# Two transformer layers in one kernel: the order of the last norms, the slot scores and three output operations

## The chip, the cores and the metric

One core of a Trainium2 chip. The time is device microseconds of one launch; the kernel before took 2937.34 us (median of three runs, 2937.07 to 2941.98). One more execution was taken with a profile, and all instruction times below are from it.

## What is computed

Two layers on x (32 sequences of 64 tokens, width 512). Each layer adds a cross attention to a context (32 query heads, 8 key/value heads of 128) and a feed-forward part. The change lies in the second layer's feed-forward part, a small memory with 128 slots:

```python
query = h @ Wq.T                                   # h = layernorm'ed x, width 512 -> 64
router_scores = (query @ Wr.T) @ (aux_keys @ Wr.T).T / sqrt(48) + log_rel
top 8 of 128 slots by router_scores
w = softmax over those 8 of (query @ aux_keys.T / 8 + log_rel)
aux_out = (w @ aux_values) @ Wvd.T @ Wvu.T
norm_var = log1p(var(h)) / (mean over all tokens of log1p(var(h)) + 1e-6)
learned = gelu(h @ Wu1.T + bu1) @ Wu2.T + bu2
u = clip(norm_var * 0.5 + sigmoid(learned) * 2.5, 0, 5)
gate = sigmoid(gate_w1 * clip((u - 0.5) / 1.5, 0, 1) + gate_bias), 0 where below 0.05
out = x + h + gate * aux_out                       # x before the norm, from the residual
```

The mean of the log variances goes over all tokens, so no gate can be finished before the last norm has its variances.

## The kernel before

The 2048 tokens lie in four chunks (c = 0 to 3) of 512 tokens, each four tiles of 128 tokens. x stays in SBUF as `x_sb[c]`. An attention runs over 32 steps (g, c): eight key/value heads g, and in each the four chunks. A step projects keys, values and queries of the next step, forms the scores S, the softmax, the values po and the output products O. Large products are done by a seven-product scheme on quarter blocks (line 186 for all of them): `product` issues eight matmuls (two for each 128x256 piece at 32-bit data), and `left_sums` and `right_sums` form the extra blocks on GpSimd (lines 166 to 177).

A tile scheduler orders the instructions of each engine from priorities and dependencies; each engine then runs its own list strictly in order, and semaphores tie the lists together. Buffers come from pools: `mm_tile` has six PSUM banks, `st_tile` one double bank, used by the attention scores S and also by the slot scores pr; `m2_tile` has four SBUF buffers.

In the output products, `output_first` forms product 1 into a bank x and product 2 into another, and adds each to the residual on VectorE (`out_add`, line 592). `output_rest` forms product 4, then product 6 on top of bank x, then 5 and 3, then product 7 on top of bank x again, each followed by its add. So product 6 can only be written when the first add has read bank x. Between these adds the softmax of the next step is worked off: S scaled (L504, VectorE), mask added (L514, GpSimd), maximum over keys r2x (L525), m1x, its spread mb (L278), subtraction (L538), exponential (L540, ScalarE), sums r2s, and the multiplication on GpSimd (L546). The scaling needs qr, a power of 128x20 values on GpSimd (L229), from sums pm that TensorE folds. GpSimd's list in such a step is qr, four left sums of oT, two mask adds.

In the last three steps of the second attention (7, 1) to (7, 3), chunk c - 1 of the residual is complete (`joined`, `norm_stats`), and behind the query projection come `norm_apply(c, "d", mem_each)` and `mem_weights(c)`; the fourth chunk follows behind the last step. `norm_apply` goes over four tiles: xnd by a tensor_scalar on VectorE (L251), four transposes xtd on TensorE (L256), a copy to xnT on ScalarE (L260). With `each`, `mem_each` then takes that tile's variance (bn_stats L1002, bn_aggr L1003) on VectorE and adds xnd into x_sb on GpSimd (L1004).

`mem_weights` projects xnT to pqy (`project`, L1014), copies it to qy, projects xnT to pu (the gate's hidden layer, two halves of 256 tokens), and then does the slot scores pr (L1031) by four matmuls. The gelu gT (L1035) reads pu, pl (L1038) is its product with Wu2, lrn (L1041) the copy of that. On VectorE the two slot-score operations L1046 and L1049 read pr; max and match_replace (L1054, L1055), left (L1057) and copy_predicated (L1058) keep the eight best. `mem_softmax` takes their maximum mmx (L1069, L1070) and the exponentials (L1072, ScalarE). `mem_values` transposes them (pwt) and multiplies with the folded values (paux). In the last chunk `behind` is `mem_mean`: the log variances (L1101), their sum over all tokens by a product with ones (plv, L1103), and its reciprocal (L1104 to L1106).

`mem_gate` forms the gates, "a" for chunks 0 to 2 and "b" for chunk 3. `mem_out` divides by the softmax sums and issues for each tile one scalar_tensor_tensor, o = aux * gate + x (L1148), and its transfer out (L1151) on SP's queue. Chunks 0 to 2 keep aux in SBUF, chunk 3 in PSUM.

Of the kernel before, what the change touches and what calls it, by code (L numbers as in the profile page):

```python
# [15 lines left out]
ALU = mybir.AluOpType  # L16
AX = mybir.AxisListType

P = 128
# [11 lines left out]
TT = CH // P  # L31
# [5 lines left out]
BOT = 64  # L37
# [7 lines left out]
def tile_xattn_ffn_2_layers(ctx: ExitStack, tc: tile.TileContext, a: dict, out: bass.AP):  # L45
    nc = tc.nc
# [12 lines left out]
    def mm_tile(name):  # L59
        return psp.tile([P, CH], F32, tag="mm", name=name)  # L60

    def st_tile(name):
        return psp.tile([P, 2, CH], F32, tag="st", name=name, bufs=1)

    def m2_tile(name):
        return ap_.tile([P, CH], F32, tag="m2", name=name, bufs=4)
# [4 lines left out]
    def q_tile(name):  # L71
        return ap_.tile([P, 4, CH], F32, tag="q", name=name, bufs=1)
# [20 lines left out]
    x_sb, xnT = [], []  # L93
# [77 lines left out]
    def right_sums(t):  # L171
        b = [t[:, k] for k in range(NBLK)]
        tt = nc.gpsimd.tensor_tensor
        tt(b[4], b[1], b[0], ALU.subtract)
        tt(b[5], b[3], b[4], ALU.subtract)
        tt(b[1], b[3], b[1], ALU.subtract)
        tt(b[6], b[2], b[5], ALU.subtract)
# [68 lines left out]
    def norm_apply(c, name, each=None):  # L246

        mv, rs = norms[c]
        for t in range(TT):
            xn = m2_tile(f"xn{name}{c}_{t}")  # L250
            ins = nc.vector.tensor_scalar(  # L251
                xn, x_sb[c][:, t, :], mv[:, t, 0:1], rs[:, t : t + 1], ALU.subtract, ALU.mult
            )
            pt = mm_tile(f"xt{name}{c}_{t}")
            for k in range(KT):
                nc.tensor.transpose(  # L256
                    pt[:, k * P : (k + 1) * P], xn[:, k * P : (k + 1) * P], ident
                )
            at = (t % 2) * P
            nc.scalar.copy(  # L260
                xnT[c][:, t // 2 : 4 : 2, :, at : at + P],
                pt.rearrange("p (j k t) -> p j k t", j=2, k=2),
            )
            if each is not None:
                each(c, t, xn)
        if each is None:
            right_sums(xnT[c])
        return ins.ins

# [13 lines left out]
    def key_blocks(kT):  # L283

        return kT.rearrange("p (f e j k) -> p f e j k", f=NH, j=4, e=KH)

    class Attention:
# [174 lines left out]
        def scores(self, g, c, kT, qT):  # L462
            n = f"{self.L}_{g}_{c}"
            kT = key_blocks(kT)
            st = st_tile(f"S{n}")
            s5 = st.rearrange("p f (e w) -> p f e w", e=KH)
            for f in range(NH):
                for e in range(KH):
                    for j in range(4):
                        nc.tensor.matmul(  # L470
                            s5[j * KB : (j + 1) * KB, f, e],
                            kT[:, f, e, j],
                            qT[:, f * 4 + j].rearrange("p h q -> p (h q)"),
                            start=True,
                            stop=True,
                        )
            return st
# [454 lines left out]
    mem = {}  # L932
# [73 lines left out]
    def blocks(c, k):  # L1006
        return xnT[c][:, k].rearrange("p h w -> p (h w)")

    def mem_weights(c, behind=lambda: None):

        def project(ps, w):
            for half in range(2):
                for k in range(KT):
                    nc.tensor.matmul(  # L1014
                        ps[:, half * HC : (half + 1) * HC],
                        w[:, k, :],
                        xnT[c][:, 2 * (k // 2) + half, k % 2, :],
                        start=(k == 0),
                        stop=(k == KT - 1),
                    )  # L1020

        py = mm_tile(f"pqy_{c}")
        project(py[0:BOT], mem["wq"])
        qy = m2_tile(f"qy{c}")
        nc.vector.tensor_copy(qy[0:BOT, :], py[0:BOT, :])
        p = mm_tile(f"pu1_{c}")
        project(p, mem["wu1"])
        behind()
        pr = st_tile(f"pr{c}").rearrange("p j (t n) -> p (j t) n", t=2)
        for t in range(TT):  # L1030
            nc.tensor.matmul(  # L1031
                pr[:, t, :], qy[0:BOT, t * P : (t + 1) * P], mem["m2"], start=True, stop=True
            )
        gT = m2_tile(f"gT{c}")
        nc.scalar.activation(gT, p, AF.Gelu_apprx_tanh, bias=mem["bu1"])  # L1035
        pl = mm_tile(f"pl{c}")
        for t in range(TT):
            nc.tensor.matmul(  # L1038
                pl[:, t : t + 1], gT[:, t * P : (t + 1) * P], mem["wu2"], start=True, stop=True
            )  # L1040
        nc.vector.tensor_copy(mem["lrn"][:, c * TT : (c + 1) * TT], pl[:, 0:TT])  # L1041
        bc = [P, TT, NSLOT]
        lr = mem["lr"].unsqueeze(1).to_broadcast(bc)

        r, rr, att = (blocks(c, k).rearrange("p (t n) -> p t n", t=TT) for k in (4, 5, 6))
        nc.vector.scalar_tensor_tensor(  # L1046
            r, pr[:, :, 0:NSLOT], 1.0 / math.sqrt(RDIM), lr, ALU.mult, ALU.add
        )
        nc.vector.scalar_tensor_tensor(  # L1049
            att, pr[:, :, NSLOT : 2 * NSLOT], 1.0 / math.sqrt(BOT), lr, ALU.mult, ALU.add  # L1050
        )
        top = sm.tile([P, TT, 8], F32, tag="top", name=f"top{c}")
        for t in range(TT):
            nc.vector.max(top[:, t, :], r[:, t, :])  # L1054
            nc.vector.match_replace(rr[:, t, :], top[:, t, :], r[:, t, :], -BIG)  # L1055
        left = sm.tile([P, TT, NSLOT], U8, tag="left", name=f"left{c}", bufs=1)
        nc.vector.tensor_tensor(left, rr, r, ALU.is_equal)  # L1057
        nc.vector.copy_predicated(  # L1058
            att, left, neg[:, 1:2].unsqueeze(2).to_broadcast(bc)
        )  # L1060
        mem["att", c] = att
# [71 lines left out]
    def mem_out(name, c0, c1):  # L1133
        gate = mem["gate", name]
        sums = mem["sums"][:, c0 * TT : c1 * TT]
        nc.vector.reciprocal(sums, sums)
        nc.vector.tensor_tensor(gate, gate, sums, ALU.mult)
        for c in range(c0, c1):
            o4 = (
                q_tile(f"o{c}")  # L1140
                if c == 0
                else (o_tile if c == 1 else w_tile)(f"o{c}")[:, 0:4].rearrange("p b h w -> p b (h w)")
            )
            for t in range(TT):
                g = c * TT + t
                col = g - c0 * TT
                o = o4[:, t, :]
                nc.vector.scalar_tensor_tensor(  # L1148
                    o, mem["aux", c, t], gate[:, col : col + 1], x_sb[c][:, t, :], ALU.mult, ALU.add
                )  # L1150
                nc.sync.dma_start(out[g * P : (g + 1) * P, :], o)  # L1151


# [16 lines left out]

    norm_stats(0, "a")
    first = norm_apply(0, "a")
    att0.start()

    def behind_first(c):
        with tc.issue_after(first):
            mask_flags(c)
            if c == 0:
                key_weight()
            if c < last:  # L1180
                load_mask(c + 1)
                norm_stats(c + 1, "a")
                norm_apply(c + 1, "a")
# [6 lines left out]
        },  # L1190
        lambda c: norm_stats(c, "b"),
        lambda c: norm_apply(c, "b"),
        tail=lambda: (ffn_load_down(0), ffn_dequant(0)),
        late={(g, c): [lambda: next(pieces, None)] for g in range(1, NKV - 1) for c in range(NCH)},
    )

    def load_second():
# [14 lines left out]
        {(0, 1): [lambda: norm_apply(last, "c")], (1, 0): [lambda: mem_constants(att1.loaded)]},  # L1212
        lambda c: (mem_values(c - 1) if c > 0 else None, norm_stats(c, "d")),
        lambda c: (norm_apply(c, "d", mem_each), mem_weights(c)),
        lambda c: mem_softmax(c, att1.copied),
    )
    norm_apply(last, "d", mem_each)
    mem_weights(last, mem_mean)
    mem_gate("a", 0, last)
    mem_softmax(last)  # L1220
    mem_values(last)
    mem_gate("b", last, NCH)
    mem_out("a", 0, last)
    mem_out("b", last, NCH)


# [77 lines left out]
```

## Time and profile before

| | |
|---|---|
| Median of three runs | 2937.34 us |
| Profiled execution, its own time | 2943.32 us |
| Its span, first to last instruction | 2941.5 us |
| Mean granted TensorE clock | 0.987 |
| TensorE busy | 2838.8 us, 97% |
| VectorE busy | 1812.1 us, 62% |
| GpSimd busy | 1283.9 us, 44% |
| ScalarE busy | 820.2 us, 28% |
| First xnd of chunks 0, 1, 2, 3 | 2755.94, 2816.95, 2864.97, 2905.33 us |
| First and last L1148 start | 2926.42 us; the last ends at 2938.32 us |

Read it as one execution: starts count from the first instruction. PE is TensorE's matmuls, PEld its weight loads, DVE VectorE, ACT ScalarE, POOL GpSimd, SPq the queue that issues transfers. In a timeline a row gives the start, the length, the instruction (output <- inputs, partitions x elements) and how many of them; in brackets the idle time before it and what ended that. Line numbers are those of the kernel before.

### The profile page before, as it was taken

The page shows a single profiled execution, that of the slowest core. Times are in us where ns is not written, and L with a number is a line of the kernel's source. Part 1 is how long each engine was busy: PE and PEld are TensorE (multiplying, and loading weights), DVE is VectorE, ACT ScalarE, POOL GpSimd, SP SyncE. Part 2 cuts the span into 40 slices and gives each one's busy share as a digit, 9 for nine tenths or more (in the row PEclk, how much of TensorE's full clock was granted, in tenths as well). Part 3 has the DMA queues.
Part 4 walks back from the last instruction along what each step waited for, and adds up shares of the span by engine and source line. Part 5 has one row for each costly group of instructions (what it writes and reads, how often), then busy time and mean ns, then how long its engine had stood idle before and what let it go on. Part 6 is the DMA issues. An engine that isn't in the chain of part 4 may idle for free.

```text
span 2941.5 us, 40415 instructions
## 1 busy us (share of the span) xinstructions
PE 2838.8 (97%) x16502; PEld 2217.1 (75%) x16502; DVE 1812.1 (62%) x2752; ACT 820.2 (28%) x1397; POOL 1283.9 (44%) x932
## 2 busy tenths in 40 slices
PE   7999999999999999899999999999999999999987
PEld 5878787778887787676666677777777777787765
DVE  7667777777777766544433665555555555555565
ACT  3323333333333333211111222222222222222232
POOL 5544545454545455411222444444445353535432
PEclk9999999999999999899999999999999999999998
DMA  4111111111111111000000102120202020201001
GB/s 159 40 44 44 52 45 51 49 60 51 45 52 44 51 44 58 23 22 22 20 8 17 36 29 67 34 65 30 65 29 65 30 65 29 65 31 64 15 1 58
DMA packets 103807, 130.71 MB, mean 44 GB/s; under 512 B 8725, under 2 KB 65165, under 8 KB 103623
## 3 DMA queue, kind: packets, MB, share of 16 engines
q1 hardware_dynamic: 103047, 127.09, 13.3%
q8 instruction: 130, 2.13, 0.3%
q10 hardware_dynamic: 576, 1.05, 0.1%
q14 instruction: 54, 0.44, 0.1%
HBM read 123.92 MB, written 4.19 MB: 44 GB/s over the span
## 4 chain that ended last, share of the span: by engine, by line
PE 80%; DVE 12%; ACT 3%; issue 2%; POOL 2%; DMA 0%; DVEq 0%; ACTq 0%; POOLq 0%
PE P L186 30%; PE O L186 22%; PE pv L369 8%; PE pk L339 6%; PE pd L896 5%; PE S L470 4%; DVE part L425 2%; PE po L566 2%; DVE x L592 2%; DVE qT L419 1%; ACT q L421 1%; ACT rq L384 1%; DVE S L493 1%; PE pqy L1014 1%; DVE r2x L525 1%
## 5 line engine op out<-in xcount | busy, mean ns | idle before, releaser
L186 PE MATMUL P<-xnT,wq 128*128 128x256 f32 x3584 | 799.2, 382 | 23.4 <-ACT h L209 21.9
L186 PE MATMUL O<-wo,oT 128*128 128x256 f32 x3584 | 803.8, 382 | 4.2 <-ACT oT L574 3.3
L186 PEld LDWEIGHTS P<-xnT,wq 128*128 128x128 f32 x3584 | 678.8, 191 | 159.2 <-issue 39.2
L186 PEld LDWEIGHTS O<-wo,oT 128*128 128x128 f32 x3584 | 671.4, 190 | 118.0 <-issue 22.1
L592 DVE TENSOR_TENSOR x<-x,O 128x512 f32<-128x512 f32 (+1 forms) x448 | 368.5, 823 | 145.6 <-PE O L186 145.1
L546 POOL TENSOR_TENSOR s<-s,ib 128x512 f32<-128x512 f32 x128 | 169.6, 1347 | 489.0 <-DVE ib L278 480.5
L209 ACT COPY h<-P 128x512 f32<-128x512 f32 (+1 forms) x352 | 200.1, 573 | 365.4 <-PE P L186 354.5
L388 POOL TENSOR_TENSOR qT<-h,rq 128x512 f32<-128x512 f32 x128 | 175.4, 1370 | 277.1 <-DVE rq L387 267.2
L186 PE MATMUL P<-xnT,wgu 128*128 128x256 f32 (+1 forms) x1232 | 273.8, 382 | 0.0
L540 ACT ACTIVATE s<-s 128x1024 f32<-128x1024 f32 x64 | 67.7, 1057 | 708.1 <-DVE s L538 708.1
L186 PEld LDWEIGHTS P<-xnT,wgu 128*128 128x128 f32 (+1 forms) x1232 | 228.0, 187 | 47.1 <-issue 7.4
L229 POOL TENSOR_TENSOR qr<-qs,nhalf 128x20 f32<-128x20 f32 x32 | 113.4, 3543 | 335.0 <-DVE qs L458 335.0
L369 PE MATMUL pv<-wkv,ctxT 128*128 128x128 f32 x1984 | 238.0, 278 | 3.0 <-DVE h L401 1.7
L369 PEld LDWEIGHTS pv<-wkv,ctxT 128*128 128x128 f32 x1984 | 226.2, 192 | 14.0 <-issue 8.6
L384 ACT COPY rq<-h 64x512 f32<-64x512 f32 x256 | 157.9, 617 | 245.3 <-DVE h L401 242.9
L339 PE MATMUL pk<-ctxT,wkv 128*128 128x512 f32 x496 | 223.1, 592 | 0.0
L419 DVE TENSOR_TENSOR qT<-h,P 128x512 f32<-128x512 f32 x128 | 83.9, 674 | 170.4 <-PE P L186 170.4
L885 POOL TENSOR_TENSOR hT<-h,h 128x512 f32<-128x512 f32 (+1 forms) x48 | 55.6, 1179 | 283.4 <-DVE h L878 263.7
L339 PEld LDWEIGHTS pk<-ctxT,wkv 128*128 128x128 f32 x496 | 94.1, 190 | 92.9 <-issue 89.9
L896 PE MATMUL pd<-wd,hT 128*128 128x512 f32 (+1 forms) x352 | 155.0, 592 | 0.0
L386 DVE TENSOR_TENSOR h<-h,cosT 128x512 f32<-128x512 f32 x128 | 90.0, 703 | 105.0 <-ACT rq L384 105.0
L878 DVE TENSOR_TENSOR h<-h,P 128x512 f32<-128x512 f32 (+1 forms) x96 | 59.6, 640 | 151.9 <-PE P L186 103.7
(235 smaller groups left out, 3234.4 us busy)
## 6 DMA issues: line engine op xcount, KB each, us to landing
ctxT<-in_ctxT SPq DMA_DIRECT2D x62, 1024.0 KB
wq<-in_L_wq SPq DMA_DIRECT2D x32, 256.0 KB
wo<-in_L_wo SPq DMA_DIRECT2D x32, 256.0 KB
wq<-in_L_wqT SPq DMA_DIRECT2D x32, 256.0 KB
wo<-in_L_woT SPq DMA_DIRECT2D x32, 256.0 KB
wgu<-in_qweight_gu SPq DMA_DIRECT2D x40, 128.0 KB
out<-o SPq DMA_DIRECT2D x16, 256.0 KB
x<-in_x SPq DMA_DIRECT2D x12, 256.0 KB
```

The lines of the kernel that those rows point to most:

```text
L186: nc.tensor.matmul(pv[0:w, m, :], left[:, l, k, m * P : m * P + w], right[:, r, k, :], start=(first and m == 0 and k == 0), stop=(k == 1), ...
L209: nc.scalar.copy(t[size], ps[size])
L229: nc.gpsimd.tensor_tensor(dst, src, nhalf[:, : src.shape[-1]], ALU.pow)
L339: nc.tensor.matmul(ps, wkv[:, k, 0, :], ctxT[:, k, :], start=(k == 0), stop=(k == KT - 1))
L369: nc.tensor.matmul(ps[:, t * HD : (t + 1) * HD], ctxT[:, k, t * P : (t + 1) * P], wkv[:, k, 1, :], start=(k == 0), stop=(k == KT - 1),)
L384: nc.scalar.copy(t[lo:hi, 1], src[HD - hi : HD - lo])
L388: nc.gpsimd.tensor_tensor(dst(None), dst(x), dst(t[:, 1]), ALU.add)
L419: nc.vector.tensor_tensor(q, xv, yv, ALU.add)
L470: nc.tensor.matmul(s5[j * KB : (j + 1) * KB, f, e], kT[:, f, e, j], qT[:, f * 4 + j].rearrange("p h q -> p (h q)"), start=True, stop=True,)
L546: nc.gpsimd.tensor_tensor(sv[:, f], sv[:, f], ib[:, f * W : (f + 1) * W].unsqueeze(1).to_broadcast([P, KH, W]), ALU.mult,)
L592: self.added = nc.vector.tensor_tensor(dst, dst, src, ALU.add).ins
L896: nc.tensor.matmul(p, hT[0:w_, t, tk * P : (tk + 1) * P], wd[i][0:w_, t, :], start=(t == 0), stop=(t == len(tiles) - 1),)
```

## The change

Three edits. In `norm_apply` with `each`, all four tiles are scaled, transposed and copied first, and `each` is called for the four tiles behind that loop. In `mem_weights`, `behind()` and the four matmuls of the slot scores pr are issued between the two halves of pu. In `mem_out`, tile 0 of chunks 0, 1 and 2 is formed on GpSimd by two operations, aux * gate in place and then the addition of x, in place of one operation on VectorE.

```diff
     def norm_apply(c, name, each=None):
 
         mv, rs = norms[c]
+        tiles = []
         for t in range(TT):
             xn = m2_tile(f"xn{name}{c}_{t}")
...
-            if each is not None:
+            tiles.append(xn)
+        if each is not None:
+            for t, xn in enumerate(tiles):
                 each(c, t, xn)
-        if each is None:
+        else:
             right_sums(xnT[c])
         return ins.ins
...
-        def project(ps, w):
+        def project(ps, w, between=None):
             for half in range(2):
+                if half == 1 and between is not None:
+                    between()
                 for k in range(KT):
...
         p = mm_tile(f"pu1_{c}")
-        project(p, mem["wu1"])
-        behind()
         pr = st_tile(f"pr{c}").rearrange("p j (t n) -> p (j t) n", t=2)
-        for t in range(TT):
-            nc.tensor.matmul(
-                pr[:, t, :], qy[0:BOT, t * P : (t + 1) * P], mem["m2"], start=True, stop=True
-            )
+
+        def scores():
+            behind()
+            for t in range(TT):
+                nc.tensor.matmul(
+                    pr[:, t, :], qy[0:BOT, t * P : (t + 1) * P], mem["m2"], start=True, stop=True
+                )
+
+        project(p, mem["wu1"], scores)
...
-                nc.vector.scalar_tensor_tensor(
-                    o, mem["aux", c, t], gate[:, col : col + 1], x_sb[c][:, t, :], ALU.mult, ALU.add
-                )
+                if name == "a" and t == 0:
+
+                    aux = mem["aux", c, t]
+                    nc.gpsimd.tensor_scalar(aux, aux, gate[:, col : col + 1], None, ALU.mult)
+                    nc.gpsimd.tensor_tensor(o, aux, x_sb[c][:, t, :], ALU.add)
+                else:
+                    nc.vector.scalar_tensor_tensor(
+                        o, mem["aux", c, t], gate[:, col : col + 1], x_sb[c][:, t, :],
+                        ALU.mult, ALU.add,
+                    )
                 nc.sync.dma_start(out[g * P : (g + 1) * P, :], o)
```

## The prediction

> **What bounds the kernel.** First the page: the totals say that TensorE works nearly all the time.
>
> ```profile
> span 2941.5 us, 40415 instructions
> PE 2838.8 (97%) x16502; PEld 2217.1 (75%) x16502; DVE 1812.1 (62%) x2752; ACT 820.2 (28%) x1397; POOL 1283.9 (44%) x932
> ```
>
> The change touches only the last 186 us (2755.9 to 2941.5), so I read that stretch by the chain of waits and by the timeline of each engine. First, the stage behind chunk 0's last norm (TensorE, VectorE, GpSimd; columns: start, length, instruction, then idle before it):
>
> ```profile
> 2774.14 2.01 PE L566 MATMUL po<-s,v 32*128 32x256 f32 x32
> 2780.02 3.62 PE L186 MATMUL O<-wo,oT 128*128 128x256 f32 x16
> 2783.57 1.93 PE L470 MATMUL S<-qT,kT 128*32 128x256 f32 x32
> 2785.43 8.93 PE L186 MATMUL O<-wo,oT 128*128 128x256 f32 x40
> ...
> 2783.62 1.44 DVE L592 TENSOR_TENSOR x<-x,O 128x512 f32<-128x512 f32 x2
> 2790.49 1.25 DVE L525 TRANSPOSE_TENSOR_REDUCE r2x<-s 128x32 f32<-128x1024 f32 x1 [2.34 <-POOL s L514]
> ...
> 2779.41 3.54 POOL L229 TENSOR_TENSOR qr<-qs,nhalf 128x20 f32<-128x20 f32 x1 [16.82 <-DVE qs L458]
> 2787.96 2.49 POOL L514 TENSOR_TENSOR s<-s,mask 128x512 f32<-128x512 f32 x2
> ```
>
> TensorE has no gap in the 40 matmuls of products 4, 6, 5, 3, 7. VectorE adds products 1 and 2 at 2783.62, long before r2x, which waits for GpSimd's chain: qr, four left sums of oT (1.27 each), two mask adds. Chunk 0's stage is TensorE's; in chunk 1, 61.2 us later, the chain of waits runs through this GpSimd chain and VectorE's list behind r2x, and TensorE idles 4.64 us before the next transposes.
>
> Next, the timelines of VectorE and GpSimd where they collide:
>
> ```profile
> 421.35 0.74 DVE L745 SCALAR_TENSOR_TENSOR scales_down<-scales_down,pidx 30x512 f32<-30x512 bf16 x1
> 422.13 1.38 DVE L744 CAST scales_down<-scales_down 30x512 bf16<-30x512 f32 x1
> 423.54 1.64 DVE L745 SCALAR_TENSOR_TENSOR scales_down<-scales_down,pidx 30x512 f32<-30x512 bf16 x1
> ...
> 421.49 3.15 POOL L546 TENSOR_TENSOR s<-s,ib 128x512 f32<-128x512 f32 x2 [8.95 <-DVE ib L278]
> ```
>
> The same scalar_tensor_tensor takes 0.74 or, issued under a GpSimd operation, 1.64, ending 0.54 after it; the cast is held likewise (0.42 alone at 420.16). GpSimd's pair takes 3.15 instead of 2.5. They take turns, one operation each.
>
> Last, TensorE's clock and the end, by windows (length, PE, PEld, DVE, ACT, POOL busy, PEclk, DMA share, GB/s):
>
> ```profile
> 2886.00:2887.00 1.00, 0.14 (x1) 0.14 (x2) 0.93 (x3) 1.00 (x3) 0.00 (x0) 1.00 0.00 0
> 2888.00:2889.00 1.00, 1.00 (x3) 0.82 (x4) 0.02 (x1) 1.00 (x5) 1.00 (x1) 0.50 0.00 0
> 2934.00:2935.00 1.00, 0.18 (x1) 0.00 (x0) 1.00 (x3) 0.00 (x0) 0.00 (x0) 1.00 0.98 375
> ```
>
> After an idle 2.07 us (2884.8 to 2886.9) the granted clock falls to 0.50 for 3.4 us (2887.9 to 2891.3). In the tail the output transfers already fill 16 engines at 375 GB/s.
>
> **The change, part by part.** The order of the built instructions (no times) decides more than the diff: the scheduler moves three further things. (a) S of the next step (16 matmuls) goes from behind products 1 and 2 to right behind the gate's projection pu. (b) On VectorE, behind the S scaling (L504), come r2x, m1x and mb, and only then the add of product 1; before, the adds of 1, 2 and 4 preceded r2x. (c) The copy lrn, which waits for pl, moves from before the second slot-score operation (L1049) to behind the top-k list. ScalarE's order is unchanged.
>
> *Chunk 0: +6.2.* The norm first: tile 1's scaling now waits for GpSimd's x add of tile 0, tile 3's for that of tile 1; the last scaling ends about 2760.2 instead of 2761.24. Half clock until 2765 makes that 1.0 worth 0.5 in pqy's end (4.93 there, 3.67 in chunk 3 at full clock). From pqy's end at 2766.75: first half of pu, pr, second half (3.66 + 1.94), S 1.86 (covers the gelu's 2.1 of table load and activation but 0.2), pl 1.0, po 1.95, pm 0.25: qs at 2777.75. The top-k list, ready for lrn at 2775.2, is ahead of pl's end. So qr starts 1.4 earlier (2778.0) and r2x with it, at 2789.05. TensorE: pv 3.7, products 1 and 2 3.6, product 4 1.8: done at 2786.7. Product 6 writes product 1's bank and must wait for its add: r2x 1.2, m1x 0.1, mb 0.75, add 0.6, so 2791.7. New stall: 5.0, with pwt, paux and the next pk queued behind it on TensorE. Less 0.5 and less the 0.27 idle before pl that S now covers (I take 0 to 0.3): 4.5 net. The clock will fall in a 5 us gap, as it did after 2.07; running on at half speed for 1.7 to 5.1 us costs 0.85 to 2.55; I take 1.7. Nothing later absorbs it: pk, P and the quarter adds of step (7,3) follow TensorE up to xnd.
>
> *Chunk 1: +1.0.* Same stall, but here VectorE's list sets the end. r2x 1.4 earlier; behind it stand adds 1, 2 and 4 too (3 x 0.6), and the exp's wait (1.2) covers one 0.6 add instead of a 1.2 one: 2.4 longer. Bounds 0 to 2.
>
> *Chunk 2: -0.2.* Xnds 0 to 2 and one statistic come first; but GpSimd's add waits when xnd 1 ends, so by the turns above xnd 2 and xnd 3 are held one add each and the last ends as before: 0 (if VectorE keeps its place, -1.1). With the stall gone before it, TensorE idles about 1 us instead of 4.64 and should be warm: pqy 3.67 for 5.42, -1.8. Against that, nothing stands between pu and pl but the gelu now: pl, po, the oT copies on ScalarE and product 1 come 1.1 later. The new 2.15 gap could also pull the clock down under po, by the rows above: 0 to 1.5, I take 0.5.
>
> Here a rule can be weighed. The row says that 2.07 us idle cost the clock. The Trainium skill (TensorE: Matmul & The Clock Gate, Part 1) says that only gaps of over some 3.4 us do; that disagrees with the row. By the rule the 0.5 is 0 and the sum 0.5 lower; I keep the row.
>
> *Chunk 3: -1.5.* The norm 0 as in chunk 2. The slot scores start 1.75 earlier (pr behind pu's first half and plv), but pl ends at 2922.85 instead of 2920.71 and lrn now stands before the maximum: mmx starts at 2923.0 instead of 2924.92. The b gate's offset and its exp now lie behind mmx (0.3). The a gates are ready 1.5 earlier.
>
> *Outputs: +2.2.* VectorE loses three of twelve L1148 (3 x 0.66), GpSimd gains three scalings and three adds. An add is 1.27 (all 128x512 rows). A one-input scaling is in no row: below, 0.66 (identity's affine select, 0.30 for 128 elements, against 0.59 for a 192-element add, scaled by length); above, the add's 1.27. I take 0.66, the row with one input. Each L1148 reads two SBUF tensors, as L745 does, so they take turns: L1148 0.65, then six turns of (GpSimd 0.66 or 1.2, L1148 0.54), two more L1148, 0.5 for the b gate, four of 0.68: the last ends 14.1 behind the gate; before it was 11.9 (2926.4 to 2938.3). So +2.2, +4.0 by the upper price. SP's queue gives the same: its second transfer now waits for GpSimd's third operation (4.3 behind the gate), and the other 13 or 14 stand behind that; 15 transfers at 0.7 from 5.2, and the 1.5 from last byte to end, give 17.2 against 15.1. Without turns, and with the cheap scaling, it would be +0.4.
>
> The Trainium skill (GPSIMD Engine Reference, 3.1) gives 769 ns for a one-input loop over 512 elements. By it the tail would be +2.5.
>
> **Sum:** 6.2 + 1.0 - 0.2 - 1.5 + 2.2 = +7.7. On the profiled execution's 2943.32 (1.8 beyond its span) that is 2951.0. That execution lies 6.0 above the median of the runs shown, 2937.34, whose spread is 2937.07 to 2941.98; so I put the same difference on the median: 2945.0.
>
> **Rivals.**
> *Not slower: product 6 isn't held.* Place: its wait on the add. It decides if r2x can come 5.0 us sooner against TensorE. For it: the gate's path is shorter. Against: qr 3.54, four sums and two mask adds are fixed rows between qs and r2x, and VectorE's listed order puts the add behind. Price: chunk 0 becomes -0.4, chunk 1 -1.4; the idle before chunk 2 and its half clock come back (+1.8): sum +0.5, 2937.8.
> *Turns go VectorE's way.* If xnds run on while GpSimd waits, each norm gains 1.1 (0.5 in chunk 0): sum about +4.5, 2941.8. For: xnd 2 at 2758.09 went ahead of an add issued 0.07 later. Against: L387 at 439.65, right behind L386, was held 1.1.
> *All dear.* Scaling at 1.27 (+1.8), no warm clock in chunk 2 (+1.8): +11.3, and slow products in chunk 1 0.8 more: 2949.4.
>
> **How the numbers follow.** Forecast 0.62 (own range +4.5 to +11), not held 0.10, VectorE's turns 0.18, all dear 0.10. Of the forecast 0.5, all of the dear case and a third of the VectorE case lie beyond 5.9 us, 0.2%, about what a measurement of this kernel tells from no change: slower 0.67, same 0.29, faster 0.04. The range leaves out most of "not held" and the far end of the dear: 2938.8 to 2950.5.
>
> **What would show it.** Right: an idle of about 5 us before the second of the O groups in steps (7,2) and (7,3), released by the add L592; PEclk at 0.50 after it; L1148 at 1.5 to 1.8 in turn with GpSimd; no output transfer moving but one for 3 to 4 us. Wrong: O running through with r2x still late; L1148 at 0.66 beside GpSimd; the last xnd 1 us earlier in every chunk.

## The result, and the profile after

Six runs of the changed kernel gave a median of 2949.8 us (2946.58 to 2951.02), six of the kernel before 2940.31 us (2937.07 to 2942.91): ratio 1.0032, 95% interval 1.0019 to 1.0045. It is slower by 9.5 us. The profiled execution took 2950.76 us, its span is 2948.9, 7.4 more than before's.

First the page of the changed kernel. It tells almost nothing: TensorE 2.9 us busier, GpSimd 9.2.

```profile
span 2948.9 us, 40420 instructions
PE 2841.7 (96%) x16502; PEld 2220.2 (75%) x16502; DVE 1816.4 (62%) x2749; ACT 820.3 (28%) x1397; POOL 1293.1 (44%) x938
```

So again the timeline behind chunk 0's last norm (the lines that answer to those of before; L595 is the add that was L592, L528 is r2x, L517 the mask add):

```profile
2771.10 1.93 PE L473 MATMUL S<-qT,kT 128*32 128x256 f32 x32
...
2780.21 5.35 PE L186 MATMUL O<-wo,oT 128*128 128x256 f32 x24
2790.93 8.53 PE L186 MATMUL O<-wo,oT 128*128 128x256 f32 x32 [5.37 <-DVE x L595]
...
2788.01 1.25 DVE L528 TRANSPOSE_TENSOR_REDUCE r2x<-s 128x32 f32<-128x1024 f32 x1 [5.07 <-POOL s L517]
...
2790.13 0.65 DVE L595 TENSOR_TENSOR x<-x,O 128x512 f32<-128x512 f32 x1
...
2785.50 2.47 POOL L517 TENSOR_TENSOR s<-s,mask 128x512 f32<-128x512 f32 x2
```

Products 1, 2 and 4 run through. Then TensorE stands for 5.37 us: product 6 waits for the add of product 1. TensorE had product 1 ready at about 2782, but its add (the L595 at 2790.13) stands on VectorE's list behind r2x, which waits for GpSimd's second mask add. Behind the stall the clock is down (windows of 1 us; the clock is the third figure from the right):

```profile
2789.00:2790.00 1.00, 0.00 (x0) 0.00 (x0) 0.93 (x3) 0.00 (x0) 0.00 (x0) 1.00 0.00 0
2791.00:2792.00 1.00, 1.00 (x3) 0.82 (x4) 1.00 (x2) 0.00 (x0) 0.00 (x0) 0.50 0.00 0
2794.00:2795.00 1.00, 1.00 (x7) 0.87 (x6) 0.99 (x3) 0.00 (x0) 0.00 (x0) 1.00 0.00 0
```

The same happens one step later (5.37 at 2858.12). The chain of waits there, in order of time (start, length, what):

```profile
2853.95 1.23 POOL s L517
...
2855.20 1.26 DVE r2x L528
...
2857.40 0.58 DVE x L595
...
2858.12 7.34 PE O L186 x24
...
2865.49 0.70 DVE x L595
...
2870.45 1.03 POOL rsd L229
```

GpSimd, then VectorE up to the held add, then TensorE's products, then the last adds and the statistics: the chain crosses from VectorE's list to TensorE at the held add and comes back. In the kernel before, TensorE had idled at the end of this stage, ahead of chunk 2's transposes; now it comes to them without a wait (before, then after):

```profile
2865.66 1.94 PE L256 MATMUL xtd<-ident,xnd 128*128 128x128 f32 x8 [4.64 <-DVE xnd L251]
```
```profile
2872.20 1.06 PE L257 MATMUL xtd<-ident,xnd 128*128 128x128 f32 x8
```

Last the tail, VectorE and GpSimd (L1162 is VectorE's output, L1159 and L1160 GpSimd's scaling and addition):

```profile
2930.49 0.75 DVE L1162 SCALAR_TENSOR_TENSOR o<-xnT,g_gatea,x 128x512 f32<-128x512 f32 x1
2931.23 1.11 DVE L1162 SCALAR_TENSOR_TENSOR o<-xnT,g_gatea,x 128x512 f32<-128x512 f32 x1
2934.96 1.23 DVE L1125 TENSOR_SCALAR g_sgb<-g_sgb 128x4 f32<-128x4 f32 x1
2936.10 1.83 DVE L1162 SCALAR_TENSOR_TENSOR o<-xnT,g_gatea,x 128x512 f32<-128x512 f32 x1
2941.94 2.73 DVE L1162 SCALAR_TENSOR_TENSOR o<-paux,g_gateb,x 128x512 f32<-128x512 f32 x4 [0.24 <-DVE g_gateb L1145]
...
2930.55 3.95 POOL L1159 TENSOR_SCALAR xnT<-xnT,g_gatea 128x512 f32<-128x512 f32 x2 [13.10 <-DVE g_ub L1132]
2934.47 2.90 POOL L1160 TENSOR_TENSOR o<-xnT,x 128x512 f32<-128x512 f32 x2
```

and the transfers, by windows (the last two figures are the DMA share and GB/s):

```profile
2932.00:2933.00 1.00, 0.62 (x1) 0.50 (x2) 1.00 (x4) 0.33 (x1) 1.00 (x2) 0.50 0.67 262
2933.00:2934.00 1.00, 1.00 (x2) 0.34 (x1) 1.00 (x3) 0.00 (x0) 1.00 (x1) 0.50 0.00 0
...
2938.00:2939.00 1.00, 0.41 (x1) 0.00 (x0) 1.00 (x3) 0.00 (x0) 1.00 (x1) 1.00 0.99 379
```

One output leaves, then none for four microseconds: the second transfer on SP's queue is that of GpSimd's first tile, done at 2935.9. From 2937 the 15 others follow each other at the full rate.

The table gives the profiles by stages (all but p_scale's, whose stages are those of before up to the last gate): from the first xnd of a chunk to that of the next, from chunk 3's to the first output operation, and from there to the end of the span. Within the stages profiles compare to a few tenths, but for the clock; the time of the first xnd itself differs by up to 5 us between executions, before anything that the change touches.

| profile | chunk 0 | chunk 1 | chunk 2 | chunk 3 | tail | sum |
|---|---|---|---|---|---|---|
| before | 61.01 | 48.02 | 40.36 | 21.09 | 15.08 | 185.56 |
| after | 66.15 | 50.00 | 39.63 | 19.36 | 18.41 | 193.55 |
| e_norm | 57.98 | 44.78 | 37.34 | 20.75 | 15.13 | 175.98 |
| e_scores | 68.87 | 50.39 | 38.98 | 20.51 | 15.13 | 193.88 |
| e_out | 61.55 | 48.30 | 40.52 | 21.08 | 18.51 | 189.96 |
| e_order | 59.62 | 45.39 | 39.69 | 19.36 | 18.45 | 182.51 |
| e_warm | 58.81 | 45.62 | 36.52 | 21.08 | 15.10 | 177.13 |
| e_outq | 60.98 | 46.07 | 40.15 | 21.08 | 17.50 | 185.78 |
| e_last | 60.80 | 44.76 | 38.84 | 19.35 | 15.09 | 178.84 |
| e_late | 58.01 | 46.38 | 41.08 | 19.35 | 15.15 | 179.97 |
| e_lastwarm | 57.94 | 44.73 | 35.73 | 19.36 | 15.12 | 172.88 |
| e_best | 57.95 | 44.74 | 35.73 | 19.37 | 15.12 | 172.91 |

From the first xnd on the change costs 8.0 us; the first xnd came 0.6 earlier, which leaves the 7.4 of the span.

### The profile page after: what moved, and what is told of

The parts are those of the page before. It is cut to its first block, busy times and chain, and to the rows that moved or that the text cites. A ratio compares the mean times of both kernels' runs of the same rounds, so it can differ in the third digit from the quotient of the medians.

```text
span 2948.9 us, 40420 instructions
## 1 busy us (share of the span) xinstructions
PE 2841.7 (96%) x16502; PEld 2220.2 (75%) x16502; DVE 1816.4 (62%) x2749; ACT 820.3 (28%) x1397; POOL 1293.1 (44%) x938
## 4 chain that ended last, share of the span: by engine, by line
PE 81%; DVE 12%; ACT 3%; issue 2%; POOL 2%; DMA 0%; DVEq 0%; ACTq 0%; POOLq 0%
PE P L186 29%; PE O L186 23%; PE pv L372 8%; PE pk L342 6%; PE pd L899 5%; PE S L473 4%; PE po L569 2%; DVE part L428 2%; DVE x L595 2%; DVE qT L422 1%; ACT q L424 1%; DVE S L496 1%; ACT rq L387 1%; DVE r2x L528 1%; PE pqy L1019 1%
## 5 line engine op out<-in xcount | busy, mean ns | idle before, releaser
L186 PE MATMUL O<-wo,oT 128*128 128x256 f32 x3584 | 806.8, 383 | 14.1 <-DVE x L595 10.7
L595 DVE TENSOR_TENSOR x<-x,O 128x512 f32<-128x512 f32 (+1 forms) x448 | 368.2, 822 | 149.3 <-PE O L186 148.9
```

The lines of the kernel that those rows point to most:

```text
L186: nc.tensor.matmul(pv[0:w, m, :], left[:, l, k, m * P : m * P + w], right[:, r, k, :], start=(first and m == 0 and k == 0), stop=(k == 1), ...
L595: self.added = nc.vector.tensor_tensor(dst, dst, src, ALU.add).ins
```

## The experiments

### Each part alone

**e_norm**: `norm_apply` of the changed kernel in the kernel before; the rest as before.

```diff
-            if each is not None:
+            tiles.append(xn)
+        if each is not None:
+            for t, xn in enumerate(tiles):
                 each(c, t, xn)
```

> The norm edit alone on the kernel before. Theory (the whole loss is the slot scores' move and the outputs; the norm's order is a small gain): last xnd 1.3 us earlier in chunk 0 and 0.35 in chunks 2 and 3, no idle inside the O products, sum -0.5 to -1.5 against before, ratio 0.9995 to 0.9998. Rival A (the four x adds on GpSimd, now in one bunch behind the variances, push qr and the left sums back, and that is what holds the add): the O groups of the last steps show an idle of several us here too, +3 to +5 us, ratio 1.001 to 1.002.

Measured: 2933.08 us against 2941.6, ratio 0.9976 (0.9967 to 0.9986). The last xnd came as early as expected, but three stages are 3.0 to 3.2 us shorter. Rival A is out: no idle inside the products. The gain is far over what the theory had, because the clock never fell in the norms of chunks 0 and 1 (pqy, the group of 16 matmuls behind the norm):

```profile
2759.52 3.67 PE L1017 MATMUL pqy<-xnT,fc 128*64 128x256 f32 x16
```

in chunk 0, and 3.67 in chunk 1 too, against 4.93 and 5.14 before. In chunk 2 pqy took 4.33 for 5.42 and the products 12.47 for 14.15.

**e_scores**: the new `project` with `scores` between its halves, for all chunks; nothing else.

```diff
-        project(p, mem["wu1"])
-        behind()
...
+        project(p, mem["wu1"], scores)
```

> The slot scores' move alone. Theory: S of the next step follows pu, r2x is queued ahead of the add of product 1, TensorE idles 5.4 us at product 6 in each of the two steps and runs on at half clock. From after's stages without the norm's gain: chunk 0 +5.6, chunk 1 +2, chunk 2 -0.4, chunk 3 -1.4, outputs 0: +5.8 us, ratio 1.0020. Rival A (the stall needs the norm's new order): no idle over 1 us before the O matmuls, -1.5 us. Rival B (the early S does harm by its 1.9 us ahead of pl and po alone): no idle, but +2 to +4 in chunks 0 and 1.

Measured: 2948.29 us, ratio 1.0024 (1.0014 to 1.0034); stalls of 5.37 and 5.38 before the same products, released by the add:

```profile
2789.74 9.01 PE L186 MATMUL O<-wo,oT 128*128 128x256 f32 x32 [5.37 <-DVE x L592]
```

Rivals A and B are out: the move alone makes the stall. Its stages sum to 8.3 over before, not 5.8; chunk 0's 68.87 has a pqy of 5.83 and products at half clock, again the clock's share.

**e_out**: tile 0 of chunks 0 to 2 on GpSimd as in the changed kernel; nothing else.

```diff
+                if name == "a" and t == 0:
+                    aux = mem["aux", c, t]
+                    nc.gpsimd.tensor_scalar(aux, aux, gate[:, col : col + 1], None, ALU.mult)
+                    nc.gpsimd.tensor_tensor(o, aux, x_sb[c][:, t, :], ALU.add)
```

> The three output tiles on GpSimd alone. Theory: stages up to the gate as before; scalings take about 2 us each in turn with VectorE, SP's second transfer waits for the third GpSimd operation (5.4 us behind the gate), 15 transfers of 0.69 follow: +3.3 us from gate to end, ratio 1.0011. By the prediction's price of the scaling (0.66) it is +2.2, ratio 1.0007. Rival (the tail of after is long because its gates came earlier than the softmax b and its exp, which now lie between the outputs): +1 or less, ratio 1.0003.

Measured: 2944.18 us, ratio 1.0009 (1.0000 to 1.0018); the tail is 18.51, 3.4 more than before, with the gates where before had them. The rival is out.

### The stall: only VectorE's list changed

**e_order**: the changed kernel, and r2x of the last four steps queued behind the adds of products 1 and 2. Only VectorE's list differs from the changed kernel's: by the traces TensorE, ScalarE and GpSimd run through the same order, with S early.

```diff
             self.out_add(c, 0, 0, self.out_product(g, c, oT, 2))
+            self.second = self.added
...
-            behind(2)
+            if self.L == 1 and g == NKV - 1:
+                with tc.issue_after(self.second):
+                    behind(2)
+            else:
+                behind(2)
```

> The changed kernel with one constraint: in the last four steps r2x is queued behind the adds of products 1 and 2. S stays early; only VectorE's list differs. Theory (the add's place behind r2x is the cause): no idle before product 6, no half clock behind it; chunk 0 60.0 to 60.5 (after 66.15, before 61.01), chunk 1 46.5 to 47.5 (after 50.00, before 48.02), chunk 2 39.6 to 41 (its gap may return and with it the half clock), tail as after; about 8 us less than after, 0 to -1 against before, ratio 0.9995 to 1.0002. Rival B (the early S itself, or the bank of product 1 held by something else): the idle stays at 5 us or moves to the next product, ratio 1.003 as after.

Measured: 2939.99 us, ratio 1.0003 (0.9995 to 1.0012), where the changed kernel had 1.0032.

```profile
2778.08 10.53 PE L186 MATMUL O<-wo,oT 128*128 128x256 f32 x48
2790.47 1.99 PE L186 MATMUL O<-wo,oT 128*128 128x256 f32 x8 [1.86 <-DVE x L595]
```

The stall of 5.37 is gone with nothing moved on TensorE; 1.86 of it comes back one product later, where product 7 waits for the add of product 6, which r2x still precedes. So the stall is the place of one add of 0.65 us on a list. The two stages fell by 6.5 and 4.6 us, and part of that is not the stall: pqy, which the constraint does not move, ran at full clock here in both, 3.67 for the changed kernel's 4.89 and 5.93. Of the eleven executions eight took 2938.7 to 2942.2 us, at a mean clock of 0.988 or 0.989, and three 2947.6 to 2949.0, at 0.985 or 0.986; none of those three was profiled, so what held them stays open.

### The clock

The norm had gained 3 us a stage, where its xnds explain 1.3. **e_warm** tests whether the rest is the clock, without touching any other engine: before's kernel, with TensorE doing filler work in the norm's gaps.

```diff
             pt = mm_tile(f"xt{name}{c}_{t}")
+            if name == "d" and c < NCH - 1:
+                for _ in range(((14, 5, 0, 8), (14, 5, 0, 8), (28, 0, 7, 0))[c][t]):
+                    nc.tensor.transpose(pt[:, 0:P], ident, ident)
```

> The kernel before with filler work on TensorE alone: transposes of the identity into the bank of the next xtd, 14 before the first tile of chunks 0 and 1 (28 in chunk 2), 5 and 8 before later ones, all inside gaps in which TensorE waits for xnd. No other engine's list changes. Theory (what the norm's gaps cost is the clock: a stretch of 3.41 us that is less than about half busy is followed by half clock): pqy 3.67 instead of 4.93, 5.14 and 5.42, no granted clock under 1.00 between the first xnd and pu in chunks 0 to 2; each of these stages 1.5 to 2 us shorter, -4 to -6 in all, ratio 0.9980 to 0.9987. Rival (pqy is slow for another reason, such as xnT coming late half by half): pqy stays at 4.9 to 5.8, ratio 1.000 or above.

Measured: 2933.24 us, ratio 0.9976 (0.9965 to 0.9986): with 89 useless transposes more, the kernel is 7 to 8.5 us faster (by the ratio and by the medians).

```profile
2754.88 2.02 PE L257 MATMUL xtd<-ident 128*128 128x128 f32 x17
2757.13 0.66 PE L259 MATMUL xtd<-ident,xnd 128*128 128x128 f32 x4 [0.23 <-DVE xnd L251]
...
2762.53 3.23 PE L1017 MATMUL pqy<-xnT,fc 128*64 128x256 f32 x14
```

The gap of 2.17 is filled but for 0.23, xnds come no earlier than before, and pqy runs at 0.23 a matmul (before 0.31). The stages are 2.2, 2.4 and 3.8 shorter, all above the expected 1.5 to 2; in chunk 2 the products ran at full clock too, 12.47 for 14.15.

### The output tiles

**e_outq**: e_out with the three GpSimd tiles' transfers placed in SP's queue behind the fifth, sixth and ninth of VectorE's.

```diff
+                if name == "a" and t == 0:
+                    held.append((g, o))
+                    continue
                 nc.sync.dma_start(out[g * P : (g + 1) * P, :], o)
+                done += 1
+                if name == "a" and done in (5, 6, 9):
+                    gp, op = held.pop(0)
+                    nc.sync.dma_start(out[gp * P : (gp + 1) * P, :], op)
```

> The three output tiles on GpSimd alone, as before, but their transfers stand in SP's queue where GpSimd will be done: behind the fifth, sixth and ninth of VectorE's. Theory (both the turns and the queue cost): transfers start and go on from 1.5 us behind the gate, the end follows VectorE's last output, 14.2 + 3.2 = 17.4 behind the gate against 18.5 with the other order and 15.1 before: +2.3, ratio 1.0008. Rival A (only the queue costs): 15.1 to 15.5, ratio 1.000. Rival B (only the turns cost): 18.5, ratio 1.0011.

Measured: tail 17.50, as the theory had it to 0.1; the time is 2944.32 us, ratio 1.0008 (0.9999 to 1.0017). The median does not tell it from e_out (one microsecond is 0.03%); the stage does. Transfers now start 1.5 us behind the gate and go on, but the last output operation still ends 14.2 behind it. So 2.4 of the 3.4 are VectorE's turns and 1.0 is the queue.

**p_scale**: before, and from the b gate on eight scalings and four additions of 128x512 on GpSimd into a scratch tile.

```diff
+        if name == "b":
+            for i in range(8):
+                nc.gpsimd.tensor_scalar(scr, x_sb[c0][:, i % TT, :], gate[:, i % TT : i % TT + 1], None, ALU.mult)
+            for i in range(4):
+                nc.gpsimd.tensor_tensor(scr, scr, x_sb[c0][:, i, :], ALU.add)
```

> The kernel before with extra work on GpSimd from the b gate on: eight scalings 128x512 of x into a scratch tile, then four additions of the same size; the first run beside the last four outputs (aux in PSUM, x in SBUF), the rest alone on an idle chip. It measures prices, and its end is longer by them. The prediction's price for a scaling alone is 0.66, its upper bound 1.27; from the changed kernel's rows of 1.97 in turn with VectorE I now expect 1.5 to 1.9 alone, and the addition 1.27. If an output whose aux lies in PSUM takes no turns, L1148 stays at 0.68 beside them and the scaling at its lone price; if any VectorE operation with an SBUF input takes turns, L1148 shows 1 to 2.

The operations by tile (name, count, shortest, median and longest ns), and VectorE's four outputs that ran beside the first two scalings:

```profile
L1141 POOL TENSOR_SCALAR scr<-x,g_gateb x8: 1562/1562/1570, 2935.0 to 2946.6; 128x512 f32<-128x512 f32 x8
L1143 POOL TENSOR_TENSOR scr<-scr,x x4: 1259/1262/1262, 2948.3 to 2952.3; 128x512 f32<-128x512 f32 x4
```
```profile
2935.07 2.73 DVE L1154 SCALAR_TENSOR_TENSOR o<-paux,g_gateb,x 128x512 f32<-128x512 f32 x4 [0.24 <-DVE g_gateb L1137]
```

A scaling costs 1.56 us alone (one execution), more than the addition with its two inputs (1.26). Beside operations with aux in PSUM it costs 1.57, and those take 0.68 each as before: no turns there. In the changed kernel, beside outputs with both inputs in SBUF, it took 1.97.

### What can be kept

**e_last**: the norm edit, the slot scores amid pu in chunk 3 only, outputs on VectorE.

```diff
-        project(p, mem["wu1"], scores)
+        project(p, mem["wu1"], scores if c == NCH - 1 else None)
+        if c < NCH - 1:
+            scores()
```

> The norm edit in all chunks, the slot scores amid pu in chunk 3 only, all outputs on VectorE. Theory: chunks 0 to 2 as with the norm edit alone (58.0, 44.8, 37.3), no idle inside the O products; chunk 3 to the first output 19.4 instead of 20.8, tail 15.1: 1.4 less than the norm alone, ratio 0.9965 to 0.9978 against before. Rival (what chunk 3 gained in after came from something else): 20.8, no gain over the norm alone.

Measured: 2934.07 us, ratio 0.9973 (0.9965 to 0.9982). Chunk 3 took 19.35 for 20.75, as expected. The time shows no gain over e_norm all the same; a gain of 1.4 us, 0.05%, would be too small to see in it. Between the two profiles e_last's sum is even 2.9 longer: chunk 0 gave away 2.8, and chunk 2 another 1.5 with its products at 13.96 for 12.47. The instructions in chunk 0 are those of e_norm, and the norm came just as early:

```profile
2757.85 1.30 PE L257 MATMUL xtd<-ident,xnd 128*128 128x128 f32 x8 [0.91 <-DVE xnd L252]
2759.81 1.09 PE L257 MATMUL xtd<-ident,xnd 128*128 128x128 f32 x4 [0.66 <-DVE xnd L252]
2760.83 6.01 PE L1019 MATMUL pqy<-xnT,fc 128*64 128x256 f32 x16
```

The clock fell at 2758.77 here and did not in e_norm.

**e_late**: as e_last, with `c >= 2` in place of `c == NCH - 1`.

```diff
+        project(p, mem["wu1"], scores if c >= 2 else None)
```

> The norm edit in all chunks, the slot scores amid pu in chunks 2 and 3, all outputs on VectorE. Against the kernel with the scores amid pu in chunk 3 only it tells what the move is worth in chunk 2, where no S of a next step fills TensorE. Theory: pl waits 2.1 for the gelu (0.18 without the move), so pl, po and the products come 1.7 to 1.9 later, and nothing gives it back: chunk 2 at 39 to 40.5 against 37.3 to 38.8, in all 1.7 more, ratio 0.9978 to 0.9990. Rival (the earlier slot scores pay as in chunk 3): chunk 2 at 36 to 37.5, ratio 0.9968.

Measured: 2934.5 us, ratio 0.9985 (0.9976 to 0.9993): chunk 2 at 41.08 against 38.84 and 37.34, on the theory's side and 0.6 beyond it, and the rival is out. The stage is not the move alone: pqy took 5.60 here and 4.53 in e_last, the products 12.47 here and 13.96 there. What the move itself does is in one line:

```profile
2878.08 1.25 PE L1048 MATMUL pl<-fc,gT 128*128 128x1 f32 x8 [2.10 <-ACT gT L1045]
```

pl waits 2.10 for the gelu, 0.18 without the move: in this chunk, where no S of a next step stands behind pu, the scores had been the cover of the gelu.

**e_lastwarm**: e_last with fillers, (14, 5, 0, 4) in chunks 0 and 1, (28, 0, 0, 2) in chunk 2.

```diff
+                for _ in range(((14, 5, 0, 4), (14, 5, 0, 4), (28, 0, 0, 2))[c][t]):
+                    nc.tensor.transpose(pt[:, 0:P], ident, ident)
```

> The norm edit, the slot scores amid pu in chunk 3 only, all outputs on VectorE, and the filler transposes of the identity in the norm's gaps of chunks 0 to 2. Theory (xnd order and clock are two separate gains): pqy 3.67 in every chunk; chunks 58, 45, 36, 19.4, tail 15.1: 12 us below before's 185.6 from the first xnd on, ratio 0.9955 to 0.9968. Rival (the norm's new order had gained only by the clock, so that fillers leave nothing to it): 177 as with the fillers alone, ratio 0.9973 to 0.9978.

Measured: 2931.06 us, ratio 0.9966 (0.9954 to 0.9978), stages 57.94, 44.73, 35.73, 19.36, 15.12: 12.7 below before's sum. The rival is out: against e_warm the norm's order is worth 0.8 to 0.9 in each of chunks 0 to 2.

**e_best**: e_lastwarm with eight more fillers between po and the O products of the last step.

```diff
                 ps = mm_tile(f"O{which}_{self.L}_{g}_{c}")
+                if self.L == 1 and g == NKV - 1 and c == NCH - 1 and which == 1:
+                    for _ in range(8):
+                        nc.tensor.transpose(ps[:, 0:P], ident, ident)
```

> As the one with norm, chunk 3 scores and fillers, with eight more filler transposes between po and the O products of the last step, where TensorE waits 1.2 us for oT. Theory: O of the last step runs at full clock in every execution, 12.5 instead of 12.5 to 14: -0.7 in the mean, ratio 0.9952 to 0.9966. Rival (the gap is too short to matter): the same as without, within the measurement.

Measured: 2929.87 us, ratio 0.9963 (0.9951 to 0.9974). In both profiles the products took 12.46, so the fillers had nothing to mend there; whether they do in other executions stays open. By the ratios both kernels beat the kernel before by 10 to 11 us, and so, adding the 9.5, the changed one by some 20.

## Why the prediction held, point by point

The forecast, slower with +7.7 us by the profile and 2951.0 for the profiled execution, met 2950.76; the mechanism was the one named. That the figures agree to 0.3 us is luck: the terms are off by up to 1.1 us each and make up for each other, and executions of one kernel lie 4 us and more apart.

**Chunk 0, +6.2 forecast, +5.14 measured.** The stall: 5.0 forecast, 5.37 measured; shown to be the add's place by e_order. Half clock behind it: 1.7 forecast; the 32 products took 8.53 for 7.14 at full clock, so 1.4. The norm: 0.5 forecast, 1.34 measured up to pqy's end; the xnds came 1.3 earlier (1.0 forecast), and the forecast kept the clock's return where before had it, while here it came 1.4 sooner after the first xnd. S between pu and pl covers nothing more of the gelu: pl still waited 0.32, since the gelu needs the second half of pu, which now stands behind pr. Without S the part from pqy to pl is 0.26 longer. Not foreseen: wT came sooner behind pwt, 0.73 for 1.28, 0.55 less. 5.37 + 1.39 - 1.34 + 0.26 - 0.55 = 5.13.

**Chunk 1, +1.0 forecast, +1.98 measured: here a step failed.** It said that VectorE's list sets the end, with 2.4 more behind r2x. The chain of waits of the changed kernel leads from the held add through 7.34 us of TensorE's products, at half clock for part of them, to the last adds. r2x came 1.08 earlier (1.4 forecast), and from it to the first xnd it took 16.30 for 13.24, 3.06 more where the forecast had 2.4. The stall had eaten the slack that made VectorE's list the bound before, 4.64 us of idle before the transposes; what was left of the stall and the clock came through.

**Chunk 2, -0.2 forecast, -0.73 measured: two terms mis-sized, in opposite directions.** The norm, put at 0, brought pqy's start 1.1 forward, 0.34 by the last xnd and the rest by transposes at full clock; the warm clock gave 1.75 as forecast (3.67 for 5.42); the exposed gelu, put at 1.1, cost 2.1, as pl's wait of 2.10 shows. The clock under po did fall (3.11 for 2.01, 0.5 forecast), but the wait for oT behind it was 0.9 shorter and the products 0.2.

**Chunk 3, -1.5 forecast, -1.73 measured**, and 1.40 in e_last, where the norm edit is in the comparison already.

**Outputs, +2.2 forecast, +3.33 measured: the scaling's price was the term.** VectorE's last output ended 14.2 behind the gate, 14.1 forecast, by luck: the scaling behind that sum was priced at a third of what it took. What came out longer is the queue. GpSimd's third operation ended at 5.4 instead of 4.3, since a scaling took 1.97 in turn and 1.56 alone, where the prediction took 0.66 and had 1.27 as its upper end. The row it went by, affine select, was the wrong neighbour. The 769 ns of the Trainium skill (GPSIMD Engine Reference, 3.1), which the page gives as the best case of a loop over 512 elements, is half of what p_scale measured.

**The rivals.** "Not held" is out by the trace. "Turns go VectorE's way" was half right: the norm's gain was larger than the forecast gave it, but in chunks 2 and 3 VectorE won only 0.35 by its turns; the rest of chunk 2's gain was the clock. "All dear" came nearer to the scaling's price with 1.27, and had chunk 2 cold, which was warm.

**The step from profile to median** failed: the 6.0 taken off came from three runs, whose median was 2937.34; the six runs beside the changed kernel's have 2940.31 (29 later ones 2941.6). Of the 4.8 by which 2945.0 lies below the 2949.8 measured, 3.0 are this, and 1.8 are the difference itself, 9.5 for 7.7.

**The size that the prediction missed altogether** was one that it touched: with all xnds first, it gave the norm edit 0.5 in chunk 0 and nothing elsewhere, counting on a cold clock. In e_norm the clock stayed up. The order makes that likelier and does not decide it: over the norms of chunks 0 and 1, fillers aside, pqy took 3.67 in 6 of 10 stages with the new order (after, e_norm, e_order, e_last, e_late) and in 1 of 10 with the old (before, e_scores, e_out, e_outq, p_scale).

## What to carry to other kernels

When TensorE's work is moved forward, look at what the scheduler then puts ahead on the other engines' lists: a short add that frees a bank, queued behind an operation that waits for a third engine, stops TensorE for that engine's whole chain, and one ordering constraint took it from 5.37 us to 1.86. Before moving work out of a slot, ask what it covered there: the slot scores hid the gelu. A gap on TensorE costs its own length and, when it leaves too little work in a stretch of 3.41 us, one to two microseconds more; closing half a gap, or filling it with useless products, can be worth more than the gap.

## What the runs showed of the hardware

**The clock is decided on a fixed grid.** In each of twelve profiles (all but p_scale) I took the times at which the granted clock changed from 2737 us on. Within a profile they all lie on one grid of 3.413 us, and its offset differs from execution to execution (0.19 in before, 1.63 in after, 0.15 in e_norm, 0.80 in e_last, modulo 3.413). Take TensorE's busy share in each stretch of the grid that ends before the first output. At full clock, of 26 stretches under 0.40 busy all were followed by half clock; of 34 between 0.40 and 0.55, 14; of 106 between 0.55 and 0.90, three (0.55 to 0.62); of 407 above, three (0.95). All six of these exceptions hold pl's one-column products, but 38 other stretches over 0.55 with such products kept the clock, so the busy share is not the whole condition. From half clock it came back behind all 25 stretches over 0.95 busy, 9 of 17 between 0.75 and 0.95, and none of 24 below. The Trainium skill (TensorE: Matmul & The Clock Gate, Part 1) calls the window free-running and 3413 ns long, and the grid agrees; its condition of an idle window does not: a gap of 2.17 us was enough in before and after, where the grid left a stretch 0.19 and 0.36 busy around it, and not in e_norm, where it split the same gap into stretches 0.59 and 0.51 busy.

This fits the 2.8 us by which e_norm and e_last differ in chunk 0 with the same instructions: in e_last the grid left a stretch 0.46 busy there. It may also be some of the 4 to 12 us between executions of one kernel, in which a longer time goes with a lower mean clock (before beside e_last: 0.988 or 0.989 up to 2941, 0.986 or 0.987 above). With fillers chunks 0 to 2 are the same to 0.01 us in e_lastwarm and e_best.

**Turns on SBUF.** VectorE's outputs with both tensors in SBUF took 1.08 to 1.83 where GpSimd held them, for 0.74; even a 128x4 operation took 1.23, for 0.17. With aux in PSUM nothing was held (0.68 beside a scaling of 1.57).
